# Local attention layers: norms through logarithm and exponential, masks on 64 rows, a normalisation on ScalarE, loads in parts, a new instruction order

## The chip, the cores and the metric

The kernel runs on one core of a Trainium2 chip. Its engines work from queues of their own and meet through semaphores: PE (TensorE, matrix products, with PEld for its weight loads), DVE (VectorE), ACT (ScalarE), POOL (GpSimd), and SP (SyncE), which issues most DMAs. The metric is the device time of one execution in microseconds (us). The profile is one execution, recorded by the hardware profiler.

## The reference

The reference chains four stages on a batch of 4 rows of 512 tokens with 128 features: a gated convolution with a scan, a mixture of experts, grouped-query attention, and six layers of local attention with a feedforward each. The change lies in the last stage. Its mathematics, cut to what matters:

```python
DEPTH = 6; HEADS = 16; DIM_HEAD = 64; WINDOW = 32; QK_SCALE = 8.0

def l2norm(t):
    return t / jnp.maximum(jnp.linalg.norm(t, axis=-1, keepdims=True), 1e-12)

def attn_layer(x, Wqkv, qs, ksc, Wo):
    q, k, v = jnp.split(x @ Wqkv, 3, -1)          # then split into 16 heads
    q = l2norm(q) * qs
    k = l2norm(k) * ksc
    q = q * cos * scale + rotate_half(q) * sin * scale
    k = k * cos * inv + rotate_half(k) * sin * inv
    sim = jnp.einsum('bhwie,bhwje->bhwij', bq, bk2) * QK_SCALE
    sim = jnp.where(mask, -jnp.finfo(sim.dtype).max, sim)
    attn = jax.nn.softmax(sim, -1)
    out = jnp.einsum('bhwij,bhwje->bhwie', attn, bv2)
    return out @ Wo

def ffn_layer(x, g, bln, W1, b1, W2, b2):
    xn = (x - mu) / jnp.sqrt(var + 1e-05) * g + bln
    a, gate = jnp.split(xn @ W1 + b1, 2, -1)
    return a * jax.nn.gelu(gate, approximate=False) @ W2 + b2
```

Each query of a window of 32 sees the keys of its own window and of the one before it. Both layers add their input to their output.

## The kernel before

**Chunks and turns.** In the local stage one unit of work is a chunk: 128 tokens of one batch row in one layer, so 6 layers x 4 rows x 4 chunks = 96 chunks (class `Chunk`). The work of a chunk is cut into steps with a name each, and the order of all instructions of all engines is written out by hand: `in_order` ties each instruction to the one before it on its engine. The tuple `TURN` is that order for one turn. In turn i the entry `(lag, step)` runs the step for chunk i minus lag, so a turn works on five chunks: it takes the products of the newest chunk, turns and scores the one before, does the softmax of the second, weighs the values of the third and projects the fourth. The first three chunks are handled in the list `MIDDLE`, interleaved with the end of the stage before; 93 turns follow; the list `LAST` ends the work.

**The steps of a chunk.** `query_up(j)` (L1173) makes one of four 128x512 products: queries (j 0, 1) and keys (j 2, 3), eight heads each. `square` (L1180, ACT) squares it for the norms, `rotate_parts` (L1192 and L1196, DVE) multiplies it by cosines and sines, `rotate_sum` (L1206, POOL) adds the two, `squares` (L1209, DVE) sums the squares of each head. `least_norms` (L1217, DVE) bounds the sums from below and `invert_norms` (L1223, POOL) raises them to the power of minus one half: once for queries (`rn`), once for keys (`rk`). `scale` (L1235, POOL) multiplies the keys by theirs; the queries' norms go into the softmax instead. `turn_up` and `turn_down` transpose (L211, PE) and copy (L860) to `qT` and `kT`; `window` (L1277, POOL) copies the last 32 keys of the chunk before. `value` (L1251) and `keep` (L1257, ACT) make the values and copy them to `vr`, of which there are three; `spread` (L1267 to L1271, SP) copies `vr` by ten DMAs to `vk`, so that every block of 32 queries finds its 64 keys' values, for which it also reads the last 32 rows of the chunk before.

`mask` (L1305) writes the masks into the scores' bank with two matmuls against an identity, and `scores` (L1317) adds 128 small products on top. `largest` (L1329, DVE) takes the maxima, `bias` (L1335) multiplies by the queries' norms, `exponentials(g)` (L1345, ACT) makes four exponentials with their sums, g from 0 to 3. `invert` (L1353) and `divide` (L1357, POOL) normalise, `flip_up` and `flip_down` transpose (L1370) and copy to `pT` (L860), `weigh` (L1393) multiplies by the values, `lift` copies (L860), `output` (L1417) projects and `add` (L1425) adds to the residual `sA`.

**Who copies.** `COPIES` gives, for each of eight copies and each of the four chunks of a row, ACT (`a`) or DVE (`v`).

**The feedforward** of a row is a generator (`feedforward`, L1427) whose parts are put between the entries of `TURN` at the places in `FEED`; its eight parts fall into three of four turns. It transposes and copies (`fn`, L1432), takes statistics (L195 to L198, and a power on POOL, L187), normalises (L203, DVE), transposes again, and makes three gate products (L1445) with Gelus (L1450), three products (L1456) and three that add up (L1466).

**Buffers that matter.** PSUM has two buffers for products (`mm`: queries, values, the output, the feedforward), two for transposes (`tr`), one for the scores (`S`) and one for the weighed values (`o`).

**Weights.** `weights(l)` (L1112) issues five DMAs for a layer at once, at the turn in which the third row of the layer before begins; eight products on POOL (L1138, `tables_of`) make its rotation tables in the same place.

## Time and profile before

| | us |
|---|---|
| median of 3 runs | 2093.36 |
| lowest, highest | 2091.99, 2095.47 |
| the profiled execution | 2094.51 |
| its span in the profile | 2092.6 |
| PE busy, of the span | 1980.7 (95%) |
| POOL busy | 1723.3 (82%) |
| DVE busy | 1613.1 (77%) |
| ACT busy | 1487.9 (71%) |

The page's first part gives busy time, share and instructions of each engine. Its second part cuts the span into 40 slices with one digit each, the busy share in tenths. The groups name line, engine, operation, what is written from what, the shape, the count, the busy time and the mean of one in nanoseconds, and after the bar the idle time ahead of them and who ended it. In a timeline, a line gives start, duration and, in square brackets, the idle time before it and its releaser. A matmul's recorded duration overlaps the next one's, so the distance from start to start is what it takes of PE.

### The profile page before, as it was taken

What the parts mean: (1) busy time and instruction counts of PE and PEld (TensorE: products, weight loads), DVE (VectorE), ACT (ScalarE), POOL (GpSimd) and SP (SyncE); (2) the same over time, 40 slices, a digit from 0 to 9 for tenths busy, and PEclk for the clock granted to TensorE, in tenths of its full rate; (3) what the DMA queues carried; (4) which work ended last, traced back from release to release, by engine and by line L of the source; (5) the groups of instructions that cost most, each with busy time, mean ns of one, the idle gap of its engine ahead of it and who ended that gap; (6) DMA issues with size and microseconds to landing.
All of it is one profiled execution on the core that took longest, in us unless ns stands there. A gap on an engine that the chain in (4) does not pass through costs nothing.

```text
span 2092.6 us, 80391 instructions
## 1 busy us (share of the span) xinstructions
PE 1980.7 (95%) x32937; PEld 1390.2 (66%) x33033; DVE 1613.1 (77%) x3343; ACT 1487.9 (71%) x4875; POOL 1723.3 (82%) x1388
## 2 busy tenths in 40 slices
PE   8989999999999999999999999999999999999997
PEld 4867777766666666666666666666666666666665
DVE  6556775778788787878877888878887788888874
ACT  2534444478787877787878778877877788887774
POOL 3646655699899889998898889998999989988882
PEclk9999999999999999999999999999999999999999
DMA  7620000012322223222232222322222322222222
GB/s 249 178 69 6 6 1 1 1 40 63 110 62 71 59 59 110 73 63 58 65 111 60 60 63 61 111 61 62 63 73 61 111 67 61 62 59 63 65 66 52
DMA packets 96665, 143.14 MB, mean 68 GB/s; under 512 B 17358, under 2 KB 41548, under 8 KB 95404
## 3 DMA queue, kind: packets, MB, share of 16 engines
q1 hardware_dynamic: 90828, 133.02, 23.6%
q8 instruction: 262, 4.29, 0.9%
q0 software_dynamic: 1472, 3.02, 0.7%
q10 hardware_dynamic: 4000, 1.97, 0.3%
q14 instruction: 103, 0.84, 0.1%
HBM read 36.36 MB, written 4.06 MB: 19 GB/s over the span
## 4 chain that ended last, share of the span: by engine, by line
PE 58%; DVE 14%; ACT 12%; POOL 6%; DMA 4%; issue 4%; SPq 2%; ACTq 0%; DVEq 0%; POOLq 0%
PE q L1173 9%; ACT lp L1345 6%; PE lv L1251 6%; PE lo L1393 5%; PE ly L1417 5%; PE tp_r L211 4%; DMA vk<-vr 4%; PE fa L1456 3%; PE fg L1445 3%; PE ls L1317 3%; PE fy L1466 3%; PE gy L1042 2%; DVE lt L1196 2%; PE lpt L1370 2%; DVE lt L1192 2%
## 5 line engine op out<-in xcount | busy, mean ns | idle before, releaser
L1345 ACT ACTIVATE lp<-ls,lnb,rn 128x64 f32<-128x64 f32 x1536 | 608.1, 437 | 28.8 <-DVE lnb L1335 28.5
L1206 POOL TENSOR_TENSOR ro<-lt,lt 128x512 f32<-128x512 f32 x384 | 484.6, 1276 | 54.0 <-DVE lt L1196 39.7
L1173 PE MATMUL q<-wqkvo,sA 128*128 128x512 f32 x768 | 383.0, 599 | 6.9 <-DVE sA L1425 4.1
L1192 DVE TENSOR_TENSOR lt<-q,rot 128x512 f32<-128x512 f32 x384 | 262.8, 684 | 152.3 <-ACT sq L1180 129.4
L1345 ACT ACTIVATION_READ_ACCUMULATOR lp<-ls,lnb,rn 128x1 f32 x1536 | 366.2, 238 | 0.0
L1223 POOL TENSOR_TENSOR rk<-rk,neg_half 128x16 f32<-128x16 f32 x96 | 278.9, 2906 | 51.3 <-DVE rk L1217 51.3
L1223 POOL TENSOR_TENSOR rn<-rn,neg_half 128x16 f32<-128x16 f32 x96 | 277.8, 2894 | 28.5 <-DVE rn L1217 26.0
L1180 ACT ACTIVATE sq<-q 128x512 f32<-128x512 f32 x384 | 234.6, 633 | 49.2 <-PE q L1173 32.8
L211 PEld LDWEIGHTS tp_r<-ident,ro 128*128 128x128 f32 x1536 | 183.2, 141 | 119.7 <-issue 92.3
L1196 DVE TENSOR_TENSOR lt<-q,rot 128x512 f32<-128x512 f32 x384 | 260.7, 679 | 0.0
L1209 DVE TENSOR_REDUCE ss<-sq 128x8 f32<-128x512 f32 x384 | 251.2, 674 | 2.3 <-ACT sq L1180 2.2
L1251 PE MATMUL lv<-wqkvo,sA 128*128 128x512 f32 x384 | 212.1, 635 | 29.1 <-DVE lt L1196 21.3
L1257 ACT COPY vr<-lv 128x512 f32<-128x512 f32 x192 | 118.9, 619 | 159.2 <-DMA vk<-vr 83.8
L211 PE MATMUL tp_r<-ident,ro 128*128 128x128 f32 x1536 | 216.7, 274 | 3.9 <-ACT lpT L860 1.1
L1393 PE MATMUL lo<-lpT,vk 64*64 64x32 f32 x12288 | 206.8, 221 | 10.5 <-issue 8.3
L1393 PEld LDWEIGHTS lo<-lpT,vk 64*64 64x64 f32 x12288 | 193.8, 136 | 29.0 <-issue 26.8
L1357 POOL TENSOR_TENSOR lp<-lp,lsum 128x512 f32<-128x512 f32 x192 | 196.4, 1044 | 10.9 <-DVE lsum L1353 10.9
L1235 POOL TENSOR_TENSOR ro<-ro,rk 128x512 f32<-128x512 f32 x192 | 196.1, 1042 | 7.4
L1173 PEld LDWEIGHTS q<-wqkvo,sA 128*128 128x128 f32 x768 | 128.5, 191 | 108.7 <-issue 46.7
L1417 PEld LDWEIGHTS ly<-oT,wqkvo 128*128 128x128 f32 x1536 | 182.3, 193 | 11.3 <-issue 10.6
L1417 PE MATMUL ly<-oT,wqkvo 128*128 128x128 f32 x1536 | 188.9, 277 | 0.3 <-ACT oT L860 0.3
L1317 PEld LDWEIGHTS ls<-kT,qT 64*32 64x32 f32 x12288 | 141.6, 105 | 44.1 <-issue 23.1
(307 smaller groups left out, 3603.2 us busy)
## 6 DMA issues: line engine op xcount, KB each, us to landing
vk<-vr SPq DMA_DIRECT2D x576, 128.0 KB
vk<-vr SPq DMA_DIRECT2D x336, 64.0 KB
wqkvo<-in_lwqkv_dram SPq DMA_DIRECT2D x6, 1536.0 KB
w<-in_ew_dram SPq DMA_DIRECT2D x20, 322.0 KB
wqkvo<-in_lwo_dram SPq DMA_DIRECT2D x6, 512.0 KB
ew<-in_ew_dram SPq DMA_DIRECT2D x8, 322.0 KB
ew<-in_ew_dram SPq DMA_DIRECT2D x8, 256.0 KB
lw<-in_lw_dram SPq DMA_DIRECT2D x6, 341.0 KB
```

The source lines that it names most:

```text
L211: nc.tensor.transpose(tp[:, c * P : (c + 1) * P], i[:, c, :], ident)
L1173: nc.tensor.matmul(q, lhsT=self.xs, rhs=self.w["qkv"][:, j * 512 : (j + 1) * 512], start=True, stop=True,)
L1180: nc.scalar.activation(self.sq[j], self.q[j], AF.Square)
L1192: nc.vector.tensor_tensor(heads(t1), heads(q), cs[:, None, :].to_broadcast([P, 8, DH]), ALU.mult)
L1196: nc.vector.tensor_tensor(swapped(t2), swapped(q)[:, :, ::-1, :], sn[:, None].to_broadcast([P, 8, 2, 32]), ALU.mult,)
L1206: nc.gpsimd.tensor_tensor(self.rot[j], *self.parts.pop(j), ALU.add)
L1209: nc.vector.tensor_reduce(self.ss[:, j * 8 : j * 8 + 8], heads(self.sq[j]), AX.X, ALU.add)
L1223: nc.gpsimd.tensor_tensor(self.r[j], self.r[j], neg_half.to_broadcast([P, HEADS]), ALU.pow)
L1251: nc.tensor.matmul(v, lhsT=self.xs, rhs=self.w["qkv"][:, (4 + j) * 512 : (5 + j) * 512], start=True, stop=True,)
L1345: nc.scalar.activation(self.P[:, i, :], self.S[:, i % 2, i // 2 * KB : (i // 2 + 1) * KB], AF.Exp, bias=self.nb[:, i : i + 1], scale=self. ...
L1393: nc.tensor.matmul(self.o[to : to + DH, odd, t0 : t0 + QB], lhsT=vk[r][lo : lo + KB, s, :], rhs=self.pT[lo : lo + KB, s, r * QB : (r + 1) ...
L1417: nc.tensor.matmul(y, lhsT=self.w["o"][:, j, :], rhs=self.oT[:, j % 2, j // 2, :], start=j == 0, stop=j == INNER // P - 1,)
```

## The change

It has six parts, all in the local stage.

1. Norms. Queries and keys are handled together in one tile of 32 columns. DVE bounds the sums and multiplies by minus one half (`x`); ACT makes y = exp(-0.5 ln(-2x)); POOL does one Newton step in four small operations, y(1.5 + x y y). The powers on POOL go. `preload_act_table_set` names the table set that has both functions, at the start of the stage before and after each feedforward's Gelus.
2. Masks. Each of the two matmuls uses 64 rows of the array instead of 128: the bands of the lower 64 rows repeat, and a 64-row selection matrix takes the place of the identity.
3. The last normalisation in `feedforward` goes from DVE to ACT (scale and bias); POOL makes the bias with two small products.
4. A layer's weights come in twelve DMAs instead of five, two after each `spread`; the rotation tables are made two products at a time in the same place.
5. `spread` issues the copies from the chunk before first.
6. Steps that had been joined are split, and `TURN`, `COPIES`, `FEED`, `MIDDLE` and `LAST` are written anew.

```diff
@@ weights @@
-        nc.sync.dma_start(w["qkv"], a["lwqkv"][l])
-        nc.sync.dma_start(w["o"], a["lwo"][l].rearrange("(c p) d -> p c d", p=P))
-        nc.sync.dma_start(w["1"], a["lw1"][l])
...
+        w["parts"] = parts = []
+
+        def part(to, of):
+            parts.append(lambda: nc.sync.dma_start(to, of))
+
+        for j in range(6):
+            at = slice(j * 512, (j + 1) * 512)
+            part(w["qkv"][:, at], a["lwqkv"][l][:, at])
...
@@ class Chunk @@
         def least_norms(self, j):
-            name = ("rn", "rk")[j]
-            self.r[j] = sm.tile([P, HEADS], F32, tag=name, name=f"{name}{self.tag}")
-            nc.vector.tensor_tensor(
-                self.r[j], self.ss[:, j * HEADS : (j + 1) * HEADS],
-                least.to_broadcast([P, HEADS]), ALU.max,
-            )
+            self.half_least(slice(j * HEADS, (j + 1) * HEADS), "nk"[j])
+            self.r[j] = self.x
+
+        def half_least(self, at, name):
+            x = sm.tile([P, 2 * HEADS], F32, tag="rn", name=f"r{name}{self.tag}")
+            self.x = x[:, 0 : at.stop - at.start]
+            nc.vector.tensor_scalar(self.x, self.ss[:, at], least, -0.5, ALU.max, ALU.mult)
 
         def invert_norms(self, j):
-            nc.gpsimd.tensor_tensor(
-                self.r[j], self.r[j], neg_half.to_broadcast([P, HEADS]), ALU.pow
-            )
...
+            self.inverse_root(self.r[j], "nk"[j])
+
+        def inverse_root(self, x, name):
+            n = x.shape[1]
+            y = sm.tile([P, 2 * HEADS], F32, tag="yn", name=f"y{name}{self.tag}", bufs=2)[:, 0:n]
+            nc.scalar.activation(y, x, AF.Ln, scale=-2.0)
+            nc.scalar.activation(y, y, AF.Exp, scale=-0.5)
+            nc.gpsimd.tensor_tensor(x, x, y, ALU.mult)
+            nc.gpsimd.tensor_tensor(x, x, y, ALU.mult)
+            nc.gpsimd.tensor_tensor(x, x, three_halves.to_broadcast([P, n]), ALU.add)
+            nc.gpsimd.tensor_tensor(x, x, y, ALU.mult)
+
+        def all_norms(self):
+            self.half_least(slice(0, 2 * HEADS), "qk")
+            self.r = [self.x[:, 0:HEADS], self.x[:, HEADS:]]
+
+        def invert_all(self):
+            self.inverse_root(self.x, "qk")
...
         def spread(self):
+            if self.c:
+                for par in range(2):
+                    nc.sync.dma_start(
+                        vk[0][par * KB : par * KB + WIN], self.last.V[P - WIN :, par]
+                    )
             for par in range(2):
                 lo = par * KB
-                if self.c:
-                    nc.sync.dma_start(vk[0][lo : lo + WIN], self.last.V[P - WIN :, par])
                 nc.sync.dma_start(vk[0][lo + WIN : lo + KB], self.V[0:QB, par])
...
         def mask(self):
             for par in range(2):
+                at = slice(par * 64, par * 64 + 64)
                 nc.tensor.matmul(
-                    S[:, par], lhsT=ident_h, rhs=bands[min(self.c, 1)], start=True, stop=False
+                    S[:, par], lhsT=row_of[at], rhs=bands[min(self.c, 1)][at], start=True,
+                    stop=False,
                 )
...
@@ feedforward @@
-        stats = statistics(n, f"f{tag}")
+        mv, rs = statistics(n, f"f{tag}")
+        ms = sm.tile([P, NC], F32, tag="ln_ms", name=f"ms_f{tag}", bufs=1)
+        nc.gpsimd.tensor_tensor(ms, mv[:, :, 0], rs, ALU.mult)
+        nc.gpsimd.tensor_tensor(ms, ms, minus_one.to_broadcast([P, NC]), ALU.mult)
         yield
-        normalise(n, n, *stats)
+        for c in range(NC):
+            nc.scalar.activation(
+                n[:, c, :], n[:, c, :], AF.Identity, bias=ms[:, c : c + 1], scale=rs[:, c : c + 1]
+            )
...
+        nc.scalar.preload_act_table_set(LOG_EXP)
...
     TURN = (
...
+        (1, "rotate_sum", 0), (3, "flip_down", 0, "e6"), (3, "flip_up", 1), (1, "rotate_sum", 3),
+        (1, "rotate_parts", 1), (2, "largest"), (1, "keep", 0), (2, "bias", nc.vector),
+        (1, "rotate_sum", 1), (1, "squares", 3), (1, "window"), (1, "squares", 1),
+        (1, "all_norms"), (3, "flip_down", 1, "e7"), (4, "output"), (4, "add"),
+        (2, "exponentials", 0), (1, "turn_up", 0), (1, "invert_all"), (2, "exponentials", 1),
+        (1, "turn_up", 1), (0, "query_up", 2), (1, "turn_down", 0, "e4"), (2, "invert", 0),
+        (0, "square", 2), (0, "query_up", 0), (0, "square", 0), (2, "exponentials", 3),
+        (3, "weigh", 0), (1, "scale"), (3, "weigh", 1), (2, "exponentials", 2),
+        (0, "rotate_parts", 2), (0, "rotate_parts", 0), (2, "value", 1), (1, "turn_up", 2),
+        (0, "query_up", 3), (1, "turn_down", 1, "e5"), (1, "turn_up", 3), (2, "divide", 0),
+        (0, "squares", 2), (2, "keep", 1), (0, "square", 3), (1, "turn_down", 2, "e2"),
+        (0, "rotate_sum", 2), (1, "mask"), (0, "query_up", 1), (2, "flip_up", 0),
+        (1, "scores", 0), (1, "turn_down", 3, "e3"), (2, "invert", 1), (2, "spread"),
+        (3, "lift", 0, "e0"), (0, "squares", 0), (0, "square", 1), (1, "scores", 1),
+        (0, "rotate_parts", 3), (3, "lift", 1, "e1"), (2, "divide", 1), (0, "value", 0),
     )
     COPIES = {
-        "e0": "aaaa",
-        "e1": "avaa",
+        "e0": "vvav",
+        "e1": "aaaa",
...
-        "e4": "avva",
-        "e5": "aavv",
-        "e6": "aavv",
-        "e7": "vavv",
+        "e4": "vvvv",
+        "e5": "vvvv",
+        "e6": "aava",
+        "e7": "aava",
     }
-    FEED = {1: (12, 36, 40), 2: (5, 12, 13), 3: (3, 11)}
+    FEED = {1: (14, 53, 58), 2: (7, 17, 18), 3: (7, 17)}
...
         if (b, c) == (2, 0) and l + 1 < DEPTH:
             ws[l + 1] = weights(l + 1)
-            list(tables_of(ws[l + 1], l + 1))
+            loads += ws[l + 1]["parts"]
+            tables = tables_of(ws[l + 1], l + 1)
...
+            if what == "spread":
+                for load in loads[:2]:
+                    load()
+                del loads[:2]
+                for _ in range(2):
+                    next(tables, None)
...
@@ _masks @@
+    first[64:] = first[:64]
+    k, to = np.arange(P)[:, None] % 64, np.arange(P)[None, :]
+    row_of = np.where(to < QB, k == to, k == QB + to % QB)
```

## The prediction, as it was made before the changed kernel ran

> **What bounds the kernel now.** I read the page first, for the busy shares and the slices.

> ```profile
> PE 1980.7 (95%) x32937; PEld 1390.2 (66%) x33033; DVE 1613.1 (77%) x3343; ACT 1487.9 (71%) x4875; POOL 1723.3 (82%) x1388
> ...
> PE   8989999999999999999999999999999999999997
> ...
> POOL 3646655699899889998898889998999989988882
> ```

> From about 440 us to 2010 us (the local layers) PE is at nine tenths or more and POOL close behind, so two engines could set the pace. To tell them apart I cut one batch (four chunks, four turns of the hand-written order) at the starts of the mask matmuls and asked for the busy time in each turn.

> ```profile
> 1382.60:1400.10 17.50, 17.42 (x317) 11.58 (x318) 14.47 (x27) 12.26 (x43) 15.09 (x12) 1.00 0.23 59
> 1400.10:1414.20 14.10, 14.03 (x310) 10.13 (x310) 10.45 (x22) 12.66 (x46) 13.87 (x11) 1.00 0.28 69
> 1414.20:1430.20 16.00, 14.84 (x313) 10.45 (x314) 13.68 (x32) 13.07 (x47) 15.82 (x13) 1.00 0.27 69
> 1430.20:1449.90 19.70, 19.17 (x323) 12.16 (x324) 16.81 (x31) 16.43 (x48) 16.68 (x14) 1.00 0.23 58
> ...
> 1039.90:1057.30 17.40, 17.30 (x318) 11.49 (x318) 14.52 (x27) 12.30 (x44) 14.65 (x12) 1.00 0.23 58
> 1057.30:1071.50 14.20, 14.15 (x309) 10.32 (x310) 10.60 (x22) 12.78 (x46) 13.98 (x11) 1.00 0.27 72
> 1071.50:1086.90 15.40, 14.68 (x313) 10.40 (x314) 12.60 (x34) 13.05 (x47) 15.32 (x18) 1.00 0.75 238
> 1086.90:1110.00 23.10, 20.76 (x324) 12.92 (x324) 15.31 (x28) 16.50 (x49) 20.15 (x16) 0.93 0.20 51
> ```

> Columns: stretch and length, then busy us of PE, PEld, DVE, ACT, POOL, granted clock, DMA share, GB/s. The first four rows are a plain batch: PE is full in the first two turns and idles 1.2 and 0.5 us in the others. The last four are the batch in which the next layer's weights and tables come in: its last turn is 3.4 us longer. Sixteen batches between 745.9 and 1835.2 us take 1089.3 us: **68.1 us a batch**, against 67.3 for the plain one.

> Is PE streaming or stretched? In its timeline, start to next start: a query or value product 0.86, four transposes 0.44, the output product 1.79, the weighing 2.09, mask and scores 2.17. A turn of 4 queries, 2 values, 6 groups of transposes and one each of the rest is 5.16+2.64+1.79+2.09+2.17 = 13.85 us. Feedforward adds nine products and two transposes, 8.62. A batch needs 4x13.85+8.62 = 64.0 us of PE. So PE is the bound, and 68.1-64.0 = **4.1 us a batch is all that ordering can win**. Where they are lost, in the same timeline and in that of ACT and DVE:

> ```profile
> 1426.16 1.10 PE L1251 MATMUL lv<-wqkvo,sA 128*128 128x512 f32 x2 [0.90 <-DVE lt L1196]
> ...
> 1433.85 1.13 PE L1251 MATMUL lv<-wqkvo,sA 128*128 128x512 f32 x2 [0.43 <-DVE lt L1196]
> ```

> ```profile
> 1419.33 0.59 ACT L1257 COPY vr<-lv 128x512 f32<-128x512 f32 x1 [1.93 <-DMA vk<-vr]
> ```

> ```profile
> 1422.46 0.87 DVE L195 BATCH_NORM_STATS2 st_f<-fn 128x6 f32<-128x128 f32 x4 [1.98 <-ACT fn L1432]
> ...
> 1429.09 3.51 DVE L203 TENSOR_SCALAR fn<-fn,mv_f,rs_f 128x128 f32<-128x128 f32 x4
> ```

> Backwards: the value product needs a buffer that DVE's rotation empties; DVE stood 1.98 us for ACT's `fn`, and ACT had stood 1.93 us ahead of the value copy L1257 until DMAs out of the old `vr` had landed. The second wait follows DVE's 3.51 us of normalisation. The four turns lose 0.2, 0.25, 1.7 and 1.1 us against 17.29, 13.85, 14.29 and 18.59.

> **The change, part by part.**

> *Norms.* Two powers leave POOL; prices of what replaces them are bracketed by these rows:

> ```profile
> L1223 POOL TENSOR_TENSOR rk<-rk,neg_half 128x16 f32<-128x16 f32 x64 | 186.0, 2906 | 33.1 <-DVE rk L1217 33.1
> L1223 POOL TENSOR_TENSOR rn<-rn,neg_half 128x16 f32<-128x16 f32 x64 | 185.2, 2894 | 19.7 <-DVE rn L1217 18.0
> ...
> L1138 POOL TENSOR_TENSOR rot<-cst,row 128x128 f32<-128x128 f32 x32 | 13.5, 466 | 0.0
> ```

> POOL's 128x512 sum takes 1.276 us and its 128x128 product 0.466: 2.1 ns a column over 0.20, so 0.26 for 128x32, and four are 1.05 (none above 0.466, so at most 1.9). POOL falls from 15.4 us a turn by 5.8-1.05 to 10.6. ACT gains a log and an exponential of 128x32, unseen here: an exponential of 128x64 with its sum recurs every 0.385 us, a copy of 128x512 lasts 0.58; I take 0.65 for both (0.2 to 1.2). DVE's two maxima (0.16 to 1.08 each) become one. All three engines stay under PE, so by itself this costs nothing; what it costs if the cover goes is the third rival. The tables: the changed program holds 49 table loads against 48, one at the first pair (1.28 us, under PE there), so log and exponential bring none per turn.

> *Final normalisation.* The 3.51 us leave DVE, and four 128x128 activations (0.29 each, the gap from an exponential to its sum) come to ACT, 1.2 us a batch, plus two small POOL products. Copies: ACT does 19 of 32 a batch, not 22 (-1.5 us). ACT's 13.6 us a turn becomes 13.6+0.65+0.3-0.4 = 14.2, DVE's 13.9 becomes about 13.1. The second PE wait loses its cause.

> *Masks.* Two 128x512 matmuls, 64 rows each, on different halves of the array. The streams show the pair with its lead at 0.53 us; one is 0.22 (from the query stream's end at 1413.95 to the second mask's start at 1414.17). The scores show that halves run together: 128 of 64 columns in 1.64 us. But PE now changes between whole and part array twice more a turn, and the weighing starts 0.09 after the stream before it ends, the score-to-transpose return costs 0.05. Net -0.07; bounds -0.2 (nothing for changes) to +0.1 (no overlap). I take -0.1, the row nearer to the like operation.

> [...]

> *Spread.* The copies of the last chunk's 32 rows are issued first, after the weighing (6.9 us into the turn), not behind copies that wait for this chunk's second value. SP takes 0.6 us an issue, ten a turn, so they are out by 8.1 and the value copy at 13.8 no longer waits: 52.1 us of ACT waits (37 times in these 16 batches) go, and with them the first PE wait.

> *Loads in parts.* Five DMAs and eight table products (3.36 us of POOL in one go at 1074.55) become two and two a turn over six and four turns, after `spread`; two issues are 1.2 us on SP, which by then has 10 copies behind it and nothing until the next weighing. The border's excess, 68.1-67.3 = 0.8 a batch, falls to 0.1.

> *The new order,* a turn without feedforward, from its first transposes (us, walked by hand with the prices above, 0.1 to 0.15 a handoff). PE: output 2.2, q/k turns 3.1, queries 4.8, weighing 6.9, value 7.8, key turn 8.2, query 3 9.1, turn 9.5, mask 9.8, query 1 10.7, flip 11.1, scores 12.8, value 13.75. ACT: exponentials from 1.15, log and exponential at 2.7 to 3.35 (DVE's minimum is there at 2.3), exponentials to 9.0, value copy 9.5, key copies 10.5 and 10.9. Margins: mask 0.5 (scores' bank), query 1 0.3, flip 0.2, value 0.2 (DVE's rotation, 6.7), key turn 2.5. Nothing stalls, but four margins are under half a microsecond. I keep the 0.2 a turn that turns without a named wait lose now, and 0.1 for margins.

> *Sum.* 64.0 - 4x0.1 + 4x0.3 + 0.1 = 64.9 us a batch, 3.2 less. The order runs 93 turns, 23.25 batches: -74 us. The hand-written end loses two powers for two shorter chains, about -1. The profiled execution took 2094.5 us (span 2092.6 and 1.9 around it), 1.15 above the median: 2019.5 there, **2018** as a median.

> **Rivals.**
> 1. *Waits move and stay.* The cured waits return as new ones: margins of 0.2 us are as thin as a handoff. Masks and borders alone: 68.1-0.4-0.7 = 67.0, 23.25x1.1 = 26 us, **2068**. Against: both named waits lose their cause.
> 2. *All waits go.* Floor with the full mask gain, 63.2: -114 us, **1980**. Against: even the quiet turns lose 0.2.
> 3. *Slower: ACT's queue.* Log and exponential stand in ACT's order between two groups of eight exponentials and wait for DVE's sums. The score bank is single: exponentials 6.2, log and exponential 0.65, squares 1.0, mask to scores 3.3, maximum and bias 1.5, handoffs 0.4 make a loop of 13.0, 0.7 under PE's turn. If DVE delivers late, each microsecond over 0.7 lengthens every turn. From 1.9 us in each turn it eats the gain (17.0 against 15.8); at 2.5, 93x0.6 = 56 us: **2149**. For: DVE waits now for ACT's squares (L1192, 82.4 us), and the two could hold each other up. Against: DVE has 2.5 us to spare in a turn.

> **How the numbers follow.** Forecast 0.64 (its own range, bounds of mask and stalls, 1980 to 2060), rival 1 0.14, rival 2 0.05, rival 3 0.15, an even sum 0.02. Range 1978 to 2075: the forecast and rival 2, most of rival 1. A measurement here tells 0.2%, 4 us. Faster 0.82, same 0.02, slower 0.16.

> **What would show it.** Batches of about 65 us; POOL under 11.5 us a turn; no DMA wait over 0.3 us before the value copy; border turns like others; the mask pair within 0.35. Wrong if PE shows waits for DVE's rotation, ACT's key copies or ACT's exponentials of over 0.5 us in every turn, or if the log's wait for the minimum passes 1 us.

## The result, and the profile after

The changed kernel took a median of 2100.0 us in 12 runs (2094.46 to 2108.41), the kernel before 2091.7 on the same chip (2089.25 to 2095.47): ratio **1.0042**, 95% interval 1.0028 to 1.0055. It became **slower by 0.4%**; forecast was 2018 us. The profiled execution took 2095.22 us, its span is 2093.3.

The page of the changed kernel, busy times and two rows of slices:

```profile
PE 1975.2 (94%) x33033; PEld 1378.9 (66%) x33033; DVE 1551.8 (74%) x3235; ACT 1517.9 (73%) x5091; POOL 1285.0 (61%) x1636
...
PE   8989999989999999999999999999999999999987
...
POOL 4636655667666667665667666676665666665642
```

POOL lost its nines, as forecast, and PE is as full as it was. Two batches of the changed kernel, four turns each (a turn is one round of the hand-written order), cut at the starts of the masks (columns as in the prediction: stretch, length, busy us of PE, PEld, DVE, ACT, POOL, granted clock, DMA share, GB/s):

```profile
1850.30:1868.20 17.90, 17.90 (x322) 11.46 (x320) 13.64 (x26) 13.02 (x47) 10.83 (x14) 1.00 0.22 53
1868.20:1882.10 13.90, 13.90 (x311) 9.88 (x310) 11.62 (x23) 12.13 (x46) 10.28 (x14) 1.00 0.33 81
1882.10:1896.50 14.40, 14.40 (x315) 10.33 (x315) 12.74 (x32) 12.71 (x47) 10.77 (x16) 1.00 0.31 75
1896.50:1915.20 18.70, 18.70 (x327) 12.10 (x326) 14.51 (x27) 17.97 (x54) 11.33 (x15) 1.00 0.24 59
...
1571.00:1592.30 21.30, 19.48 (x321) 12.40 (x320) 13.63 (x26) 13.02 (x47) 10.73 (x14) 0.92 0.18 46
1592.30:1606.30 14.00, 14.00 (x311) 9.98 (x310) 11.57 (x23) 12.18 (x46) 10.23 (x14) 1.00 0.33 78
1606.30:1624.60 18.30, 16.19 (x317) 11.28 (x316) 13.06 (x33) 12.85 (x47) 11.28 (x16) 0.91 0.25 60
1624.60:1644.10 19.50, 18.91 (x325) 12.18 (x324) 14.34 (x26) 17.97 (x54) 12.76 (x19) 1.00 0.31 83
```

The first batch takes 64.9 us, the forecast, with PE busy throughout. It is the quickest of its kind: cut four turns from every turn on, and 22 stretches hold no stop of the sort described below; their median is 66.0. The second batch does the same work, but for four small products on POOL and loads of weights in its last turn, in 73.1: two of its turns lose 3.4 and 3.9 us. Over turns 3 to 92 (22.5 batches, from mask to mask) the mean is 68.0 us a batch, against 68.2 before. So most of the gain is there in some batches and is lost in others, and what is lost shows in PE's waits from 460 to 1990 us (who waited for what: us in total, times, longest):

```profile
PE ls L1346 <- issue: 39.0, 24, 2.1
PE lo L1422 <- issue: 7.3, 14, 0.8
```

24 times PE stops in the middle of the scores, for no engine and no DMA. In the kernel before the scores did that once, for 0.7 us; the weighing did, in the same manner:

```profile
PE lo L1393 <- issue: 8.3, 13, 1.2
...
PE ls L1317 <- issue: 0.7, 1, 0.7
```

One such stop in the timeline of the changed kernel, PE alone (start, duration, what, and in brackets the idle time before it):

```profile
1147.49 0.39 PE L1333 MATMUL ls<-mask_h 64*128 64x512 bf16 x2
1147.81 1.12 PE L1192 MATMUL q<-wqkvo,sA 128*128 128x512 f32 x2
1148.77 0.60 PE L1399 MATMUL lpt<-ident,lp 128*128 128x128 f32 x4
1149.30 1.27 PE L1346 MATMUL ls<-kT,qT 64*32 64x64 f32 x102
1152.20 0.44 PE L1346 MATMUL ls<-kT,qT 64*32 64x64 f32 x26 [1.63 <-issue]
```

After 102 of 128 equal products with nothing new to wait for, PE stands 1.63 us. Three things in the trace say what it is.

*The place.* Number all instructions that the trace has of PE (weight loads, matmuls, semaphore instructions and a few others) in the order of their starts: all 24 stops come at number 193 or 194 modulo 256.

*The blocks.* The page's queue of instructions holds 263 packets, each of 16,384 bytes; PE's 67,367 instructions over 263 are 256 a packet:

```profile
q8 instruction: 263, 4.31, 0.9%
```

One of them starts at 1149.99, 0.69 us into the scores above, and takes 0.94; PE goes on at 1152.20. Of the 226 transfers in the local layers, half start within 1.1 us after PE passes the border of the block before, nine in ten within 3.8; this one came 5.5 us after. The 256 instructions of the scores pass in 1.6 us, less than the 2.2 from that start to PE's going on (2.2 to 3.1 at the 24 stops). From 460 to 1990 us the waits of PE that are put down to "issue" number 41 (48.2 us), so at most of the borders no stop shows; at these 24 one does, 39.0 us in all.

*The semaphore instruction.* For the transposes just before the scores (`flip_up` of the first half, L1399), from 1143 to 1150 us, the trace has (duration minimum, median, maximum in ns, then the first and last start):

```profile
L1399 PEldq EVENT_SEMAPHORE  x1: 1779/1779/1779, 1146.5 to 1146.5; - x1
```

and for both halves' transposes, from 460 to 1990 us:

```profile
L1399 PEldq EVENT_SEMAPHORE  x181: 51/976/1779, 463.2 to 1986.5; - x181
```

It is an instruction of PE's sequencer. Of the groups listed below only flip 0 waits for more than one engine, and only ahead of it does the trace have such an instruction: 181 at L1399 for 181 groups of transposes, none at the masks (L1333) or the scores (L1346). In the new order these transposes are the last ones before the scores that wait for several:

```
Matmult ls (mask)         [waits Activation]
Matmult q (query 1)       [waits Activation]
Matmult lpt (flip 0)      [waits PE, Activation, Pool]
Matmult ls (scores 0)     no wait
Matmult ls (scores 1)     [waits Activation]
```

In all of 92 turns that instruction ends 1.03 to 0.71 us before the scores (1.03 in the median), and 0.04 after ACT's first key copy, which frees the transposes' bank. Of 42 transfers that started after it and by the first microsecond of the scores, none came less than 1.04 us behind its end, and none at all lies between 1.9 us before the scores and their start. Over the local layers, where such a long semaphore instruction begins between the border and the transfer (20 of the 226), the transfer starts 2.7 to 5.5 us after the border, with a median of 5.0; for the others the median is 1.0. In the kernel before, the same transposes stand behind the scores and find all they need, and the last semaphore instruction ahead of the scores belongs to other transposes and ends 3.0 to 5.5 us earlier. Those of the same transposes never take more than 0.05 us there:

```profile
L1370 PEldq EVENT_SEMAPHORE  x180: 51/51/51, 464.6 to 1978.9; - x180
```

### The profile page after: what moved, and what is told of

It reads as the page before. It is cut to its first block, busy times and chain, and to the rows that moved or that the text cites. A ratio compares the mean times of both kernels' runs of the same rounds, so it can differ in the third digit from the quotient of the medians.

```text
span 2093.3 us, 80934 instructions
## 1 busy us (share of the span) xinstructions
PE 1975.2 (94%) x33033; PEld 1378.9 (66%) x33033; DVE 1551.8 (74%) x3235; ACT 1517.9 (73%) x5091; POOL 1285.0 (61%) x1636
## 4 chain that ended last, share of the span: by engine, by line
PE 85%; DVE 6%; issue 4%; ACT 3%; POOL 1%; DMA 1%; ACTq 0%; SPq 0%; DVEq 0%; POOLq 0%
PE q L1192 16%; PE lv L1274 9%; PE lo L1422 9%; PE ly L1440 8%; PE tp_r L219 8%; PE ls L1346 7%; PE lpt L1399 4%; PE fa L1489 3%; PE fy L1499 3%; PE fg L1477 3%; PE gy L1050 2%; PE gs L972 2%; ACT gp L993 2%; PE rq L944 2%; PE ls L1333 1%
## 5 line engine op out<-in xcount | busy, mean ns | idle before, releaser
L1374 ACT ACTIVATE lp<-ls,lnb,rqk 128x64 f32<-128x64 f32 x1488 | 581.4, 420 | 31.5 <-DVE lnb L1364 31.2
L1192 PE MATMUL q<-wqkvo,sA 128*128 128x512 f32 x768 | 391.6, 608 | 2.3 <-DVE sA L1448 1.6
L1374 ACT ACTIVATION_READ_ACCUMULATOR lp<-ls,lnb,rqk 128x1 f32 x1488 | 327.6, 220 | 0.0
L1199 ACT ACTIVATE sq<-q 128x512 f32<-128x512 f32 x384 | 223.0, 602 | 96.0 <-PE q L1192 76.5
L1386 POOL TENSOR_TENSOR lp<-lp,lsum 128x512 f32<-128x512 f32 x192 | 200.6, 1045 | 63.5 <-DVE lsum L1382 63.5
L219 PE MATMUL tp_r<-ident,ro 128*128 128x128 f32 x1536 | 220.9, 274 | 7.1 <-POOL ro L1267 4.4
L1251 POOL TENSOR_TENSOR rqk<-rqk,yqk 128x32 f32<-128x32 f32 x93 | 23.6, 253 | 308.0 <-ACT yqk L1250 304.1
L1346 PE MATMUL ls<-kT,qT 64*32 64x64 f32 x12288 | 161.8, 226 | 41.0 <-issue 41.0
L1267 POOL TENSOR_TENSOR ro<-ro,rqk 128x512 f32<-128x512 f32 x186 | 190.3, 1044 | 7.3
L1346 PEld LDWEIGHTS ls<-kT,qT 64*32 64x32 f32 x12288 | 140.0, 105 | 64.1 <-issue 62.2
L1192 PEld LDWEIGHTS q<-wqkvo,sA 128*128 128x128 f32 x768 | 120.8, 190 | 75.1 <-PE tp_r L219 28.4
```

The source lines that it names most:

```text
L219: nc.tensor.transpose(tp[:, c * P : (c + 1) * P], i[:, c, :], ident)
L1192: nc.tensor.matmul(q, lhsT=self.xs, rhs=self.w["qkv"][:, j * 512 : (j + 1) * 512], start=True, stop=True,)
L1199: nc.scalar.activation(self.sq[j], self.q[j], AF.Square)
L1346: nc.tensor.matmul(S[to : to + QB, par, s, :], lhsT=self.qT[lo : lo + 64, s, to : to + QB], rhs=self.kT[lo : lo + 64, s, to : to + KB], st ...
L1374: nc.scalar.activation(self.P[:, i, :], self.S[:, i % 2, i // 2 * KB : (i // 2 + 1) * KB], AF.Exp, bias=self.nb[:, i : i + 1], scale=self. ...
```

## The experiments

Ratios are to the kernel before on the same chip. On the chips of e1 to e8 the kernel before took 2112 us, some 20 more, which lie ahead of the local layers; the figures per batch, over 22.5 batches of the one profiled execution, are free of that. Stops in the scores are PE's waits for "issue" there from 460 to 1990 us, as the list above counts them. The expectations of e1 to e4 give times as on the chip of the result: against them stand ratio times 2091.7, which is 2088, 2169, 2126 and 2055 us.

| run | ratio, 95% interval | us a batch | stops in the scores |
|---|---|---|---|
| kernel before | 1 | 68.2 | 1, 0.7 |
| changed kernel | 1.0042 (1.0028 to 1.0055) | 68.0 | 24, 39.0 us |
| e1 no value copies | 0.9982 (0.9968 to 0.9996) | 67.5 | 23, 30.9 |
| e2 value copy earlier | 1.0369 (1.0342 to 1.0395) | 71.1 | 26, 45.0 |
| e3 scores split | 1.0165 (1.0147 to 1.0183) | 69.2 | 22, 11.3 |
| e4 old order, other parts | 0.9825 (0.9809 to 0.9841) | 66.4 | 0 |
| e5 flip 0 behind the scores | **0.9784** (0.9764 to 0.9804) | 65.8 | 3, 1.7 |
| e6 borders shifted | 1.0050 (1.0028 to 1.0071) | 67.9 | 23, 36.3 |
| e7 before + order of copies | 0.9995 (0.9983 to 1.0008) | 68.0 | 1, 0.2 |
| e8 before + masks | 1.0008 (0.9995 to 1.0022) | 68.0 | 1, 0.5 |
| e9 one transpose put back | 1.0141 (1.0124 to 1.0158) | 68.8 | 24, 45.0 |
| e10 e5 with powers | 1.0711 (1.0694 to 1.0729) | 74.0 | 0 |
| e11 e5, loads at once | 0.9851 (0.9835 to 0.9868) | 66.3 | 1, 0.4 |
| e12 before + copies + ACT normalisation | 0.9883 (0.9866 to 0.9899) | 67.0 | 1, 0.3 |

**e1: are SyncE's DMA issues in the way?** The first theory came from a coincidence: the late transfers started while `spread` was issuing its copies, beside issues that took 1.1 us and more instead of 0.6.

```diff
-                getattr(made[i - lag], what)(*of)
+                if not (what == "spread" and made[i - lag].l > 0):
+                    getattr(made[i - lag], what)(*of)
```

> The changed kernel with the copies of each chunk's values into the neighbouring key tiles (spread, ten SyncE DMAs a turn) left out in the layers' turns; its output is not the reference's. What is asked is whether PE's stops in the middle of the scores belong to SyncE's DMA issues. Theory A (PE's next block of instructions is fetched late because SyncE's DMA issues stand ahead of it): the 24 stops of 1.3 to 2.1 us in the scores, 39 us in all, and what they drag behind them go, fewer than 5 stops are left, time 2020 to 2060 us. Theory B (the block is late because PE's own sequencer reaches the request late, by its own semaphore waits, whatever SyncE does): at least 18 stops stay, time 2085 to 2102 us. Theory C (the loss lies with ScalarE's queue and the log and exponential, the prediction's third rival): time within 10 us of 2100.

There are as many stops as before, 24 with one just behind 1990 us: **theory A fell**. (Many of them strike other turns, since leaving out `spread` also takes away PE instructions.) They are shorter, 1.33 us against 1.62, and the transfers start 1.28 us in the median after the semaphore instruction's end, against 1.38. So the issues, or the copies' own traffic, may have a small part in it, some 0.3 us a stop; which of the two was not told apart. Stops and time are as B had them.

**e2: the value copy and SyncE's copies earlier.**

```diff
-        (3, "weigh", 0), (1, "scale"), (3, "weigh", 1), (2, "exponentials", 2),
+        (3, "weigh", 0), (1, "scale"), (3, "weigh", 1),
...
-        (0, "squares", 2), (2, "keep", 1), (0, "square", 3), (1, "turn_down", 2, "e2"),
+        (0, "squares", 2), (2, "keep", 1), (2, "exponentials", 2), (0, "square", 3), (1, "turn_down", 2, "e2"),
```

> The changed kernel with one step moved: the second value copy (keep 1) stands ahead of the third group of exponentials on ScalarE, so SyncE's eight copies that wait for it are issued some 1.5 us earlier and end before the scores begin. Theory A: the request for PE's block then comes after most of the issues, the stops in the scores shrink from 1.6 to under 1 us or go, time 2040 to 2085 us. Theory B: stops as in the changed kernel, time 2090 to 2110. Against any gain: the copy waits on PE's value product, and ScalarE's exponentials behind it would wait too; if that decides, 2100 to 2130.

The stops stayed (26), against A again, and the mask now waits for the last exponentials in nearly every turn:

```profile
PE ls L1346 <- issue: 45.0, 26, 2.1
PE ls L1333 <- ACT lp L1374: 44.1, 87, 1.5
```

So the margin of 0.5 us that the prediction gave the mask does not hold the value copy and its wait.

**e3: a product between the halves of the scores.**

```diff
-        (3, "lift", 0, "e0"), (0, "squares", 0), (0, "square", 1), (1, "scores", 1),
-        (0, "rotate_parts", 3), (3, "lift", 1, "e1"), (2, "divide", 1), (0, "value", 0),
+        (3, "lift", 0, "e0"), (0, "squares", 0), (0, "square", 1), (0, "rotate_parts", 3),
+        (0, "value", 0), (1, "scores", 1), (3, "lift", 1, "e1"), (2, "divide", 1),
```

> The changed kernel with the value product of the next chunk (0.86 us on PE, few instructions) between the two halves of the scores instead of behind them. Both theory A and B (PE runs out of instructions because 256 short matmuls go by in 1.64 us while the next block is fetched in 2 to 3 us): a fetch that starts with the scores has 0.86 us more, the stops shrink by up to that, from 39 us to about 18 us, time 2070 to 2090 us. Theory C, or a loss that has nothing to do with the density of the scores: time within 5 us of 2100, or slower by the value product's being early.

The stops shrank from 39.0 to 11.3 us, as both theories had it: how fast the instructions go by counts. But the moved steps cost more than that in new waits (69.2 us a batch), so its time says nothing on the theories.

**e4: the old order with four of the parts** (masks, ACT normalisation, loads in parts, order of the copies; the powers stay).

> The kernel before with the change's masks by 64 rows, last normalisation on ScalarE, loads and tables in parts and the order of the copies, but with its own order of steps and its powers on GpSimd. The prediction's named waits (the value copy behind DMAs, VectorE behind its own normalisation, the borders) are cured by just these parts. Theory A: the old order puts the fetch ahead of SyncE's copies, so no stops come in the scores, and the cures show: 65 to 66.5 us a batch, time 2020 to 2060 us. If the waits only move (the prediction's first rival): 2065 to 2085. If the order is needed for the cures: 2085 to 2100.

2075.3 us, ratio 0.9825: **the cures work without the new order**, and no stop comes in the scores. What was expected under A came out, but for another reason than A's.

After these four, B was sharpened to theory D: the semaphore instruction ahead of a PE instruction that waits for several engines holds PE's sequencer, and the next block is requested only past it.

**e5: the wait for several engines taken from before the scores.**

```diff
-        (0, "rotate_sum", 2), (1, "mask"), (0, "query_up", 1), (2, "flip_up", 0),
+        (0, "rotate_sum", 2), (1, "mask"), (0, "query_up", 1),
         (1, "scores", 0), (1, "turn_down", 3, "e3"), (2, "invert", 1), (2, "spread"),
...
-        (0, "rotate_parts", 3), (3, "lift", 1, "e1"), (2, "divide", 1), (0, "value", 0),
+        (0, "rotate_parts", 3), (3, "lift", 1, "e1"), (2, "divide", 1),
+        (2, "flip_up", 0), (0, "value", 0),
```

> The changed kernel with one step moved: the transposes of the first half of the probabilities (flip 0) come after the scores instead of right before them. They are the last PE instruction before the scores that waits for several engines (PE, ScalarE, GpSimd), and the trace shows a semaphore instruction of its own there on PE's sequencer, which ends 1.0 us before the scores; PE's next block of instructions is requested only after it (theory D). Without it the last such instruction stands 3 us before the scores, as in the kernel before. Theory D: the block starts to come at least 1 us before the scores, the 24 stops of 1.3 to 2.1 us in the scores go (3 or fewer are left), and 40 to 70 us with them: ratio to the kernel before 0.965 to 0.985. If the stops come from something else in the new order (rival E): 15 or more stops stay, ratio 0.998 to 1.010. If the later transposes make the weighing wait instead: no stops, but ratio over 0.99 with new waits at the weighing.

Theory D held, time and all. PE's waits, and the semaphore instructions of the same line:

```profile
PE lo L1422 <- issue: 10.0, 15, 1.1
...
PE ls L1346 <- issue: 1.7, 3, 1.3
```

```profile
L1399 PEldq EVENT_SEMAPHORE  x185: 51/51/51, 473.7 to 1984.4; - x185
```

None of them waits any more, and 36 transfers now start 0.2 to 2.9 us before the scores, where the changed kernel had five, the last at 1.9. At 0.9784 this one move beats both kernels.

**e6: the same work with the borders elsewhere.**

```diff
             self.S = S = psum("S", f"ls{self.tag}")
+            if (self.l, self.b, self.c) == (0, 1, 0):
+                for _ in range(64):
+                    nc.tensor.matmul(
+                        S[:, 0][:, 0:1], lhsT=row_of[0:64], rhs=bands[0][0:64, 0:1],
+                        start=True, stop=True,
+                    )
```

> The changed kernel with 64 matmuls of one column (128 PE instructions) put once ahead of the first mask of the second batch row, so that every later block border of 256 instructions falls 128 instructions earlier in its turn; the work per turn is the same. Theory D with blocks of 256: a turn stops in its scores where the border falls on the scores' instruction 181 or later, so the stops move to other turns: those whose border was at 52 to 127 (25 turns) stop, and none of the 24 that stopped before does. Time as the changed kernel within 0.6% (4 us for the added matmuls and a handful of stops more or fewer), ratio to the kernel before 0.999 to 1.011. Rival E (the stops belong to the work of a turn: copies, table loads, weights): the same turns stop as before.

24 turns stopped (23 of them before 2010 us), **all among the 26 whose border had stood at 52 to 127**, and none of the 25 that stop in the changed kernel (24 before 1990 us, one at 2013). Rival E is out: the turn's work does not matter, the count modulo 256 does. A batch has 2575 instructions, 15 over ten blocks, so the border wanders 15 a batch through the turn and each turn is struck in some batches: that is why quiet and costly batches stand side by side.

**e9: the wait put back, three quarters of the work left where e5 has it.**

```diff
-        (0, "rotate_sum", 2), (1, "mask"), (0, "query_up", 1),
+        (0, "rotate_sum", 2), (1, "mask"), (0, "query_up", 1), (2, "flip_one", 0),
...
-        (2, "flip_up", 0), (0, "value", 0),
+        (2, "flip_rest", 0), (0, "value", 0),
```

> The kernel with flip 0 behind the scores, with the first of its four transposes (0.11 us) put back right before the scores; it brings back the wait for PE, ScalarE and GpSimd, but a quarter of the work. Theory D (the wait for several engines holds PE's sequencer): the stops in the scores come back, 18 to 28 of them, 30 to 45 us, ratio to the kernel before 0.996 to 1.010. Rival F (what counted was the 0.44 us of transposes between mask and scores, or the place of the other three): 6 stops or fewer, ratio 0.975 to 0.988.

```profile
PE ls L1346 <- issue: 45.0, 24, 2.3
```

```profile
L1414 PEldq EVENT_SEMAPHORE  x90: 973/1246/1779, 464.2 to 1987.5; - x90
```

One transpose of 0.11 us with that wait brings 24 stops back, most of them in the same turns: it is the wait, not the work. The ratio, 1.0141, is above the expected range: the instruction ends nearer to the scores (0.70 us in the median), the stops are longer (45.0 us in all), and nine turns had a granted clock of 0.90 to 0.92 (see the last section).

**e7 and e8: single parts on the kernel before.** e7 has only the loop of e4 that issues the last chunk's copies first, e8 only the masks.

> The kernel before with only the order of the value copies changed (the last chunk's 32 rows first). The prediction's step: ScalarE's wait of 1.93 us for DMAs ahead of its value copy (52.1 us in 16 batches, 37 times) goes, and with it PE's first wait (1.2 to 1.7 us a batch): 23 batches, 25 to 40 us, ratio 0.981 to 0.988. If the wait only moves: ratio 0.996 to 1.002.

> The kernel before with only the masks by 64 rows. The prediction's step: 0.1 us less a turn on PE, 9 us, bounds -0.2 to +0.1 us a turn; ratio 0.991 to 1.004, value taken 0.996. If PE's waits stand between: ratio 0.998 to 1.002.

Neither gains. In e7 ACT's wait for the DMAs fell from 80.5 to 11.7 us, and the time stayed: PE's third turn gained 0.7 us a batch (16.0 to 15.3) and its fourth lost 0.5 (20.4 to 20.9), where PE's waits for DVE's normalisation grew (`fn`, 1.2 to 9.1 us). The wait moved. In e8 PE needs 0.11 us less a turn for the masks, as taken, and none of it arrives in the time.

**e12: both named waits cured.** The edit is e7's and the normalisation of the change's `feedforward`.

> The kernel before with the order of the value copies changed and the last normalisation on ScalarE: the cures of both waits that the prediction named (PE 1.7 and 1.1 us in the third and fourth turn of a batch), without masks, loads or the new order. If they are two covers of the same loss, each alone gives nothing (the copies alone gave 0.9995) and both together 1.2 to 2 us a batch: ratio 0.978 to 0.987. If the waits move on: 0.994 to 1.002, and the gain of the four parts in the old order (0.9825) comes from loads and masks.

1.2 us a batch, ratio 0.9883, between the two expectations: together they give what the copies alone do not, though less than taken. The normalisation alone was not run, so it is not shown whether both are needed or the normalisation would do by itself. What the four parts gain over these two in the old order (66.4 against 67.0) is left for masks and loads.

**e10: the powers in the new order.**

```diff
-            self.inverse_root(self.x, "qk")
+            for j in (1, 0):
+                nc.gpsimd.tensor_tensor(
+                    self.r[j], self.r[j], neg_half.to_broadcast([P, HEADS]), ALU.pow
+                )
```

> The kernel with flip 0 behind the scores, with the norms in the turns by two GpSimd powers of 16 columns again (2 x 2.9 us) instead of log, exponential and four small products. The prediction costed the change of the norms at nothing by itself, since all three engines stay under PE: ratio as without this edit, 0.976 to 0.984. If the new order needs the short norms (5.8 us on GpSimd in one go, 15.4 us a turn in all, ahead of the key scaling): PE waits for GpSimd in every turn, ratio 1.00 or more.

POOL's timeline, and the first of PE's waits:

```profile
1407.54 5.77 POOL L1267 TENSOR_TENSOR rqk<-rqk,neg_half 128x16 f32<-128x16 f32 x2 [1.19 <-DVE rqk L1260]
1413.28 1.04 POOL L1274 TENSOR_TENSOR ro<-ro,rqk 128x512 f32<-128x512 f32 x1
```

```profile
PE tp_r L219 <- POOL ro L1274: 101.5, 44, 3.6
```

The new order costs 8.2 us a batch more with powers than without. The 5.77 us stand in one piece ahead of the key scaling, and PE's key transposes wait for that.

**e11: loads and tables at once again.** Each layer's twelve loads and its eight table products are issued where the layer's weights are made.

> The kernel with flip 0 behind the scores, with each layer's weights and tables again issued and made in one go (twelve DMAs, eight GpSimd products of 0.42 us) at the third batch row. The prediction priced the border at 0.7 us a batch, 16 us in all: ratio 0.984 to 0.988 against 0.978 without this edit. If GpSimd, which is now some 10 us busy a turn, covers them: 0.976 to 0.981.

0.5 us a batch, 0.7% in time; the prediction had said 0.7 us.

## Why the prediction was wrong, step by step

- **What bounds the kernel, and the turn.** Right: PE is the bound, and the turn as walked comes to within 0.9 us a batch. The forecast was 64.9; the quickest stretches without a stop take that, their median is 66.0, and e5 has 65.8 in the mean. That one batch shows 64.9 to the tenth is luck of the choice.
- **The two named waits.** The mechanism was right, the size was not. In the changed kernel the value copy no longer waits for DMAs, and DVE's wait for `fn` (34.1 us before) shrank to 3.3. But in the old order the first cure alone gives nothing (e7) and both together 1.2 us a batch (e12), where the sum had 2.2 (1.7 to 0.3 and 1.1 to 0.3). That the second wait covers the first is what e7 suggests; without a run of the normalisation alone it is not shown.
- **Masks.** Right on PE, nothing in the time. The pair takes 0.32 us from its start to the next product's, as the test "within 0.35" asked. Counted like the 0.53 of the kernel before, from the end of the stream ahead of it, it is 0.42: 0.11 less, where 0.1 was taken. In e8 that is not to be seen in the time (0.9995 to 1.0022, where 0.4 us a batch would be 0.996). The 0.42 hold a stream of 0.22 (as read in the kernel before), so the lead and the changes between whole and part array take 0.20 together.
- **Norms ("by itself this costs nothing").** Wrong in what it asks. The prediction compared engines' sums per turn, where POOL lay under PE either way. e10 shows that place counts: the new order cannot be had with the powers in one piece.
- **Loads in parts.** Right within a third: 0.5 us a batch for 0.7.
- **The new order: "Nothing stalls, but four margins are under half a microsecond."** This step failed, and with it go 49 of the 70 us missed. The four margins held: PE lost 3.4 us in all to three waits of the value product for DVE, and 1.6 at one query product. What the walk left out is that PE's instructions have to arrive as well. It placed a transposes' wait for three engines a microsecond ahead of 256 instructions that take 1.6 us, and gave it a price of nothing because PE had other work in its queue meanwhile. Taking that wait away (e5) gives back 49.0 us of the 90 turns (1529.9 to 1480.9): 37.3 from stops, 4.5 from turns at a lowered clock, and 7.2 that were not traced to a cause. The forecast for these 90 turns was 22.5 x 64.9 = 1460, so 70 us were missed. The other 21 are still there in e5; its stops in the weighing (10.0 us) are among them, and the rest was not taken apart.
- **The rivals.** The slower side came true, but not by rival 3: ACT's loop did not lengthen the turn, since batches with log and exponential take 64.9 when no stop strikes. Its condition was also set too high: 1.9 us are needed to eat the gain from a turn of 15.8, the floor of rival 2; from the forecast's own 16.2 (64.9 over four), 1.5 would do. Rival 1 ("waits move and stay") named the outcome nearest, at 2068, without the mechanism. The prediction's signs of failure listed waits for DVE, ACT and exponentials; none came. The sign was a releaser called "issue", and the kernel before had 13 of them in its weighing.

## What to carry to other kernels

A hand-written order of short PE instructions has a supply of its own to keep: look for PE idle time put down to "issue", count its place modulo 256, and list which PE instructions wait for several engines. Keep the last of these that really waits well ahead of any dense run (here 256 instructions in 1.6 us), even if the engine has other work queued in between: ending 0.7 to 1.0 us ahead it cost stops, and where the last semaphore instruction ended 2.0 us ahead or more (e5, the kernel before) they were all but gone. Moving one transposes group past the scores was worth 2.6% here. And when the cure of one wait gives nothing, try it together with the cure of the next before dropping it.

## What the runs showed of the hardware that was not expected

- The cost of a border depends on the phase of the instruction count: 128 instructions more at the start moved every stop to another turn (e6). With single waits alone just before the scores, e5 has 3 stops there (1.7 us); with the semaphore instruction of 0.97 to 1.78 us, e9 has 24 (45.0 us). What that instruction does to the request for the next block the page does not say.
- A stop of about 2 us can cost some 1.5 us more in clock. After the stop of 2.11 us at 1611.66, the changed kernel's two value products take 2.07 us instead of 1.12, and that turn's granted clock is 0.91:

```profile
1611.66 0.47 PE L1346 MATMUL ls<-kT,qT 64*32 64x64 f32 x15 [2.11 <-issue]
1612.06 2.07 PE L1274 MATMUL lv<-wqkvo,sA 128*128 128x512 f32 x2
```

  It happened after 3 of the 24 stops in the changed kernel and in nine turns of e9, and in no turn of e5. The three are 1.82, 2.11 and 1.95 us long, and the granted clock is 0.50 from 1577.4 to 1580.8, from 1611.6 to 1614.9 and from 1819.8 to 1823.1; other stops as long (1.89 us before 984.29, 1.91 before 1084.34) went without, at 1.00 in the 3.6 us behind them. Summed over turns 4 to 91, PE's busy time times the missing clock is 4.5 us in the changed kernel, 13.9 in e9, 0 in e5. It is not tied to the scores: e6 with its stops lost nothing, and the kernel before lost 7.6 us in four turns, three of them behind PE's waits of 2.2 to 2.7 us for POOL where a new layer's weights come in. Why the changed kernel's times scatter over 14 us, where those of the kernel before stay within 6, is open.
